# Four graph layers on one core: per-node columns stored as rows after an on-chip transpose, and three transfers moved to other queues

## The chip, the cores and the metric

The kernel runs on one core of a Trainium2 chip. Its time is device microseconds (us) from start to end of one execution, and the smaller the better. One profiled execution with all instructions and all transfers is at hand beside the times.

The engines are named as the profile names them: PE is the matrix engine (PEld its weight loads), DVE the vector engine, ACT the scalar engine, POOL the general engine, SP the engine that only issues transfers. A transfer (DMA) is started by an instruction in the queue of SP, ACT or POOL; the transfers themselves run on 16 DMA engines that all queues share.

## The reference

`adj` is a sparse matrix of 2708 x 2708 (stored dense, with weights), `x` is 2708 x 512. Four layers follow each other; each ends with a layernorm of its input plus its result. Cut to what matters:

```python
deg = max((adj != 0).sum(-1), 1)                       # used in layer 3
# layer 0
head = (adj > 0) / sqrt(count of adj > 0 in the row)   # counts per row
x = layernorm(x + ((adj + head) @ x) / rowsum(adj + head))
# layer 1
h = x @ W_sa
s_left, s_right = h @ a_sa[0, :512], h @ a_sa[0, 512:]      # one score per node
e = where(adj != 0, exp(-leaky_relu(s_left[:, None] + s_right[None, :])), 0)
x_a = (e / (rowsum(e) + 1e-5)) @ h
x_b = adj @ (x @ W_gcnb) + b_gcnb
x = layernorm(x + sigmoid(gate_a(adj @ x, x) * x_a + gate_b(adj @ x, x) * x_b))
# layer 2: p = x; three hops p = adj @ p, each times a weight, summed
# layer 3
dinv = rsqrt(deg)
x = layernorm(x + relu((dinv * (adj + I) * dinv @ x + x) @ W + b))
```

So two things per node are made once and used much later: the two score columns of layer 1 (`rcol` below, which the kernel's third sweep adds to its exponent) and the reciprocal degree (`rdeg`, used in the last sweep).

## The kernel before

The nodes are split into two halves of 1354 and the columns of an output into ranges of 384, 384, 256 and 330. The products with `adj` use the seven-product (Strassen-Winograd) scheme on 2 x 2 blocks, so that sums and differences of adjacency blocks are needed as well. A function `sweep` does one product of the whole matrix: the first sweep is layer 0, the second is `adj @ x` of layer 1 (profile: about 430 to 815 us), the third the attention product of layer 1, and four more (`sweep2`) do the three hops and layer 3. Work is put in a list with a position, sorted, and emitted; the framework makes the order of each engine's queue and all waits from it. Each engine takes its queue strictly in order.

The loads of the adjacency, on the queue of SP, and the sums of blocks, which the second sweep also stores (`save`) for the hops:

```python
def load(ij, k):
    t = ring_tile("a" + ij)                    # one of 38 buffers
    nc.sync.dma_start(out=t[:, :n], in_=adjT[j0 : j0 + P, hi * NH + R0 : hi * NH + R0 + n])
    A[r, ij, k] = t

def comb(dst, a, b, op, k):
    nc.vector.tensor_tensor(A[r, dst, k][:, :n], A[r, a, k][:, :n], A[r, b, k][:, :n], op)
    if save:
        nc.scalar.dma_start(out=SD[m][k * P : (k + 1) * P, R0 : R0 + n], in_=A[r, dst, k][:, :n])
```

The matrix products of a sweep, and how a finished sum leaves its PSUM bank (ACT copies it, or DVE adds it):

```python
nc.tensor.matmul(B[home, c][:, :n], X[STAT[p], k][:, c * P : (c + 1) * P], A[r, MOV[p], k][:, :n], ...)
...
def copy_out(nm, home):
    for c in range(2):
        T[nm, c] = tmp(nm)
        nc.scalar.copy(T[nm, c][:, :n], B[home, c][:, :n])
```

The counts of layer 0. While one range is worked on, the count tiles of the next are loaded (`cl`), made into a 0/1 mask on ACT, and counted by small products:

```python
def count_load(R0, n, h, i):
    t = tmp("cl")                              # one of 17 buffers
    move(nc.gpsimd, t[:w, :n], adjT[j0 : j0 + w, h * NH + R0 : h * NH + R0 + n])

def count_mask(R0, n, h, i):
    nc.scalar.activation(m[:w, :n], t[:w, :n], AF.Sign)
    nc.scalar.activation(m[:w, :n], m[:w, :n], AF.Relu)

def count_tile(R0, n, h, i):
    for j, q in enumerate(tiles_of(R0, n)):
        nc.tensor.matmul(cnt[h][:wq, j : j + 1], m[...], ones_bf[:w, 0:1], ...)
```

The scores. `score` (DVE) makes them node tile by node tile, `scores_end` finishes a group of two to four node tiles and stores the two columns of each tile to memory; the reciprocal degrees are stored likewise:

```python
def scores_end(R0, h, ts):
    ...
    for k in ts:
        for j in range(2):
            nc.gpsimd.dma_start(out=SROW[R0, h][j : j + 1, k * P - R0 : ...].rearrange("a i -> i a"),
                                in_=rcol[: wt(k), h * KT + k, j : j + 1])

def end(h):                                    # in the second sweep
    ...
    nc.gpsimd.dma_start(out=DROW[h][0:1, q * P : q * P + wq].rearrange("a i -> i a"), in_=o)
```

A column lies across the partitions, one value of four bytes in each. The third sweep reads `SROW` back as a row, spread over all partitions (`rows`, on SP), the last sweep does so with `DROW`. After the second sweep's range, `done1` needs the finished sums `C` and, for the gates, these small products (`pz`) and a larger one (`ps_d`):

```python
nc.tensor.matmul(pz[:w], C[h, c][:, lo : lo + w], wab_sb[:, c, :], ...)
...
px = dense(lambda c: C[h, c][:, lo : lo + w], W[1], w)
nc.scalar.mul(y[:w], y[:w], gate[:w, t, 1:2])
move(nc.gpsimd, XB[t], y[:w])
```

Of the kernel before, what the change touches and what calls it, by code (L numbers as in the profile page):

```python
# [21 lines left out]
F32 = mybir.dt.float32  # L22
# [3 lines left out]
P = 128  # L26
EPS = 1e-5
NH = 1354
KT = 11
RANGES = [(0, 384), (384, 384), (768, 256), (1024, 330)]  # L30
RANGES0 = [(768, 256), (0, 384), (384, 384), (1024, 330)]
# [27 lines left out]
def wt(k):  # L59
    return min(P, NH - k * P) if k < KT else P  # L60
# [8 lines left out]
def gnn_kernel(ctx: ExitStack, tc: tile.TileContext, x, adjT, w_sa, a_sa, w_gcn, b_gcn, wab, bab, w_hop, w_out,  # L69
               b_out, out):  # L70
    nc = tc.nc
# [9 lines left out]
    small = ctx.enter_context(tc.tile_pool(name="small", bufs=6))  # L81
    psum = ctx.enter_context(tc.tile_pool(name="psum", bufs=1, space=bass.MemoryType.PSUM))
    dram = ctx.enter_context(tc.tile_pool(name="dram", bufs=1, space=bass.MemoryType.DRAM))

    ident = const.tile([P, P], F32, name="ident")
# [13 lines left out]
    gate = const.tile([P, NT, 2], F32, name="gate")  # L99
    rcol = const.tile([P, NT, 2], F32, name="rcol")  # L100
    rdeg = const.tile([P, NT], F32, name="rdeg")
    wab_sb = const.tile([P, 2 * DC, 2], F32, name="wab_sb")
    bab_sb = const.tile([P, 2], F32, name="bab_sb")
    vmat = const.tile([P, DC, 4], F32, name="vmat")
# [4 lines left out]
    def feature(nm):  # L109
# [4 lines left out]
    X0 = [x[h * NH + k * P : h * NH + k * P + wt(k), :] for h in range(2) for k in range(KT)]  # L114
    OUT = [out[h * NH + k * P : h * NH + k * P + wt(k), :] for h in range(2) for k in range(KT)]

    SROW = {(R0, h): dram.tile([2, w], F32, name=f"SR{R0}_{h}", tag=f"SR{R0}_{h}")
            for R0, w in RANGES for h in range(2)}
    DROW = [dram.tile([1, NH], F32, name=f"DR{h}", tag=f"DR{h}") for h in range(2)]

    X2T = {(g, h): dram.tile([D, 2 * n], F32, name=f"X2T{g}_{h}", tag=f"X2T{g}_{h}")
           for g, (_, n) in enumerate(RANGES2) for h in range(2)}
# [3 lines left out]
    SD = {m: dram.tile([NH, NH], F32, name=f"A{m}", tag=f"A{m}") for m in SUMS}  # L126
# [3 lines left out]
    def bcast(src, n):  # L130
        return bass.AP(tensor=src.tensor, offset=src.offset, ap=[[0, P], [1, n]])

    def move(queue, dst, src):

        m = dst.shape[0]
        c = m - m % 16 if m > 16 else m
        queue.dma_start(out=dst[:c], in_=src[:c])  # L137
        if c < m:
            queue.dma_start(out=dst[c:m], in_=src[c:m])

    def ring_tile(nm):
        return pool.tile([P, 384], F32, name=nm, tag="ring", bufs=RING)
# [13 lines left out]
    def bank(nm, shape=None):  # L156
        return psum.tile(shape or [P, D], F32, name=nm, tag="x", bufs=8)
# [6 lines left out]
    def at(pos, fn, hold=False):  # L164

        def go():
            n = len(nc.cur_bb.bb.instructions)
            fn()
            held.update(range(n, len(nc.cur_bb.bb.instructions)))

        events.append((pos, len(events), go if hold else fn))
# [187 lines left out]
    def sweep(base, ranges, prep=None, extra=None, done=None, first=False, late=None, sums=False, save=False):  # L359
        A, spare = {}, {}  # L360
        nk = KW
        for r, (R0, n) in enumerate(ranges):
            plain = first and r == 0
            pb = base + 7 * r - plain
# [20 lines left out]
            def comb(dst, a, b, op, k, n=n, r=r, R0=R0):  # L385
                if dst == "s3":
                    A[r, "s3", k] = ring_tile("s3")
                nc.vector.tensor_tensor(A[r, dst, k][:, :n], A[r, a, k][:, :n], A[r, b, k][:, :n], op)  # L388
                if save:
                    m = dst if dst == "s3" else {("21", "21"): "s1", ("11", "21"): "s2", ("11", "12"): "s4"}[dst, a]  # L390
                    nc.scalar.dma_start(out=SD[m][k * P : (k + 1) * P, R0 : R0 + n], in_=A[r, dst, k][:, :n])
                if sums and (dst, a) in (("21", "21"), ("11", "12")):
                    add_run(R0, int(dst == "21"), n, P, A[r, dst, k])

# [6 lines left out]
            for ij in ("11", "21", "22", "12"):  # L401
                for k in ks:
                    p, f = when[ij]
                    at(pb + p + f * k / nk, lambda ij=ij, k=k, load=load: load(ij, k))
                    if prep is not None:
                        p, f = pw[ij]
# [13 lines left out]
            for k in ks if not plain else ():  # L420
                f = 0.75 * k / nk
# [48 lines left out]
            if plain:  # L470
                for i in range(8):
                    for k in ks:
                        at(pb + i + k / nk, lambda i=i, k=k, step=plain_step: step(i, k))
                    if i % 2:
                        h, e = i // 4, i // 2 % 2
# [54 lines left out]
            for h in (1, 0):  # L530
                ts = list(range(R0 // P, (R0 + n + P - 1) // P))
# [70 lines left out]
    S = [28.0 * s for s in range(8)]  # L602


    row, run, rd = {}, {}, {}
# [3 lines left out]
    def tiles_of(R0, n):  # L609
        return list(range(R0 // P, (R0 + n + P - 1) // P))  # L610

    def count_load(R0, n, h, i):
        w = wt(i % KT)
        t = tmp("cl")
        j0 = (i // KT) * NH + (i % KT) * P
        move(nc.gpsimd, t[:w, :n], adjT[j0 : j0 + w, h * NH + R0 : h * NH + R0 + n])
        cnt[R0, h, i] = t

    def count_rows(R0, i):
# [153 lines left out]
    for k in range(KW):  # L773
        f = k / KT
# [18 lines left out]
        vec[1] = const.tile([P, D], F32, name="vec", tag="vec")  # L793
        nc.scalar.dma_start(out=vec[1], in_=bcast(b_gcn, D))

    at(S[1] - 1.0, start1)
    deg = {}

    def spread_v():
# [20 lines left out]
    def scores_end(R0, h, ts):  # L820
        q = slice(h * KT + ts[0], h * KT + ts[-1] + 1)
        m = len(ts)
        nc.vector.tensor_tensor(sc[:, q, :], sc2[:, q, 0, :], sc2[:, q, 1, :], ALU.add)
        nc.vector.tensor_scalar(neg_s[:, q], sc[:, q, 1], -1.0, None, ALU.mult)
        nc.vector.tensor_scalar(neg_s01[:, q], sc[:, q, 1], -0.01, None, ALU.mult)
        for j in range(2):
            nc.vector.tensor_scalar(gate_x[:, q, j], sc[:, q, 2 + j], bab_sb[:, j : j + 1], None, ALU.add)

        s01 = small.tile([P, 4], F32, name="s01", bufs=2)
        nc.vector.tensor_scalar(s01[:, :m], sc[:, q, 0], 0.01, None, ALU.mult)  # L830
        nc.vector.tensor_tensor(g_col[:, q], sc[:, q, 0], s01[:, :m], ALU.max)
        nc.vector.tensor_tensor(rcol[:, q, 0], g_col[:, q], sc[:, q, 0], ALU.subtract)
        nc.vector.tensor_tensor(rcol[:, q, 1], g_col[:, q], s01[:, :m], ALU.subtract)
        for k in ts:
            for j in range(2):
                nc.gpsimd.dma_start(out=SROW[R0, h][j : j + 1, k * P - R0 : k * P - R0 + wt(k)].rearrange("a i -> i a"),
                                    in_=rcol[: wt(k), h * KT + k, j : j + 1])

    def scores_over():

# [6 lines left out]
    i = 0  # L847
    for R0, n in RANGES:
        for h in (1, 0):
            for k in tiles_of(R0, n):  # L850
                def go(t=h * KT + k):
                    got1[t] = fetch(X1[t])

                at(S[1] + 0.7 + 0.95 * i, go)
                at(S[1] + 1.1 + 0.95 * i, lambda t=h * KT + k, w=wt(k): score(t, w, got1))
                i += 1
            at(S[1] + 1.12 + 0.95 * (i - 1), lambda R0=R0, h=h, ts=tiles_of(R0, n): scores_end(R0, h, ts))
    at(S[1] + 1.13 + 0.95 * (i - 1), scores_over)

    def extra1(pb, r, R0, n, A):  # L860
        ts = tiles_of(R0, n)

        def tally(h, key, w=P):

            a = A[(r,) + key]
            if (R0, h) not in deg:
                deg[R0, h] = d = tmp("deg")
                nc.vector.tensor_scalar(d[:w, :n], a[:w, :n], 0.0, None, ALU.not_equal)
            else:
                d = deg[R0, h]  # L870
                nc.vector.scalar_tensor_tensor(d[:w, :n], a[:w, :n], 0.0, d[:w, :n], ALU.not_equal, ALU.add)  # L871

        for ij, p in (("11", -0.6), ("21", 0.05), ("22", 1.05), ("12", 3.6)):
            for k in range(KW):
                at(pb + p + 0.8 * k / KT, lambda ij=ij, k=k: tally(int(ij[0]) - 1, (ij, k)))
        for h, p in ((1, 2.0), (0, 4.5)):
            at(pb + p, lambda h=h: tally(h, ("r", h), KA))
            at(pb + p, lambda h=h: tally(h, ("r32", h), 32))

        def end(h):  # L880
            d = deg.pop((R0, h))
            ps = bank("ds", [P, 4])
            for i, q in enumerate(ts):
                wq = wt(q)
                nc.tensor.matmul(ps[:wq, i : i + 1], d[:, q * P - R0 : q * P - R0 + wq], ones_f, start=True, stop=True)
            for i, q in enumerate(ts):
                wq = wt(q)
                o = rdeg[:wq, h * KT + q : h * KT + q + 1]
                nc.vector.tensor_scalar(o, ps[:wq, i : i + 1], 1.0, None, ALU.max)
                nc.vector.reciprocal(o, o)  # L890
                nc.gpsimd.dma_start(out=DROW[h][0:1, q * P : q * P + wq].rearrange("a i -> i a"), in_=o)

        at(pb + 2.6, lambda: end(1))
        at(pb + 5.2, lambda: end(0))

    def done1(p0, dp, last, R0, n, h, C, tiles):
        for i, (t, lo, w) in enumerate(tiles):
# [44 lines left out]
    def extra2(pb, r, R0, n, A):  # L942
        def rows(h):
            row[R0, h] = [tmp("row") for _ in range(2)]
            for m in range(2):
                nc.sync.dma_start(out=row[R0, h][m][:, :n], in_=bcast(SROW[R0, h][m : m + 1, :], n))

        def share(o, s, t, w):
            nc.vector.tensor_tensor(o, s, eps_col[:w, t : t + 1], ALU.add)
            nc.vector.reciprocal(o, o)  # L950
            nc.vector.tensor_tensor(o, o, gate[:w, t, 0:1], ALU.mult)

        at(pb - 1.6, lambda: rows(0))
        at(pb - 1.0, lambda: rows(1))
        at(pb + 5.2, lambda: run_sums(R0, n, 0, share))
        at(pb + 4.7, lambda: run_sums(R0, n, 1, share))
# [375 lines left out]
    for n, i in enumerate(list(nc.cur_bb.bb.instructions)):  # L1332
        p = last if n < 3 * strict else done if n in held else {}
# [44 lines left out]
```

## Time and profile before

| | us |
|---|---|
| median of 3 runs | 2961.59 |
| lowest, highest | 2958.91, 2971.53 |
| span of the profiled execution | 2972.7 |
| first to last store of the degree columns (`DR<-rdeg`, 22 transfers) | issued 498.3 to 885.6 |
| first to last store of the score columns (`SR<-rcol`, 44 transfers) | issued 499.9 to 813.3 |
| stores of the block sums (`As<-a` and `As<-s`, 160 transfers, ACT queue) | issued 428.1 to 866.9 |
| loads of all count tiles (`cl<-in_adjT`, 144 transfers, POOL queue) | issued 1.5 to 314.9 |

How the views are to be read: in a row of the waits, the engine and line that waited stand left of the arrow, what ended the wait right of it, then the total in us, how often, and the longest. A row of the windows gives for one stretch its length, then each engine's busy time (with the count of its instructions), the granted PE clock as a share of full speed, the share of time the 16 DMA engines were busy, and GB/s. A row of the timeline gives start, duration, engine, line, operation, tiles and count, and in brackets the idle time before it and what ended that.

### The profile page before, as it was taken

The page shows a single profiled execution, that of the slowest core. Times are in us where ns is not written, and L with a number is a line of the kernel's source. Part 1 is how long each engine was busy: PE and PEld are TensorE (multiplying, and loading weights), DVE is VectorE, ACT ScalarE, POOL GpSimd, SP SyncE. Part 2 cuts the span into 40 slices and gives each one's busy share as a digit, 9 for nine tenths or more (in the row PEclk, how much of TensorE's full clock was granted, in tenths as well). Part 3 has the DMA queues.
Part 4 walks back from the last instruction along what each step waited for, and adds up shares of the span by engine and source line. Part 5 has one row for each costly group of instructions (what it writes and reads, how often), then busy time and mean ns, then how long its engine had stood idle before and what let it go on. Part 6 is the DMA issues. An engine that isn't in the chain of part 4 may idle for free.

```text
span 2972.7 us, 37453 instructions
## 1 busy us (share of the span) xinstructions
PE 2878.5 (97%) x10898; PEld 1862.9 (63%) x10898; DVE 2233.1 (75%) x5666; ACT 568.1 (19%) x1105; POOL 626.1 (21%) x1116
## 2 busy tenths in 40 slices
PE   6999999999799999999999999999999999999997
PEld 4655665556565666776665666666666666665653
DVE  4898788556546866686598787887888877689886
ACT  3654300000026644462100000000000200100001
POOL 1333222011200010122302223031330312512112
PEclk9999999999899999999999999999999999999999
DMA  7676468786864342464667768566675766866652
GB/s 209 185 214 192 130 186 209 153 130 134 154 143 125 104 150 78 146 200 146 208 189 217 218 194 246 169 205 197 203 235 156 224 194 182 245 180 183 177 159 81
DMA packets 385064, 523.85 MB, mean 176 GB/s; under 512 B 66168, under 2 KB 339872, under 8 KB 384860
## 3 DMA queue, kind: packets, MB, share of 16 engines
q1 hardware_dynamic: 295944, 362.26, 43.5%
q0 software_dynamic: 48896, 120.34, 13.2%
q10 hardware_dynamic: 40020, 38.87, 6.3%
q8 instruction: 86, 1.41, 0.2%
q14 instruction: 118, 0.97, 0.1%
HBM read 432.03 MB, written 89.21 MB: 175 GB/s over the span
## 4 chain that ended last, share of the span: by engine, by line
PE 80%; DMA 7%; DVE 6%; issue 4%; POOL 1%; ACT 1%; SPq 0%; POOLq 0%; ACTq 0%; DVEq 0%
PE accu L1116 10%; PE accd L1116 10%; PE accc L1116 10%; PE ps_d L591 9%; PE accc L443 8%; PE accd L443 8%; PE accu L443 8%; PE acca L1116 5%; PE acca L443 3%; PE accr L1187 2%; DMA a<-in_adjT 1%; DVE z L1076 1%; PE acca L452 1%; PE accr L1191 1%; PE accd L452 1%
## 5 line engine op out<-in xcount | busy, mean ns | idle before, releaser
L1076 DVE TENSOR_TENSOR z<-z 128x339 f32<-128x339 f32 (+1 forms) x966 | 457.6, 506 | 13.9 <-PE accu L1116 2.5
L1134 ACT COPY q<-accu 128x338 f32<-128x338 f32 (+1 forms) x84 | 34.3, 443 | 988.7 <-PE accu L1116 988.7
L1116 PE MATMUL accc<-s,t 128*128 128x338 f32 (+1 forms) x644 | 198.6, 453 | 1.0 <-DVE s L1076 1.0
L1116 PE MATMUL accu<-z,t 128*128 128x338 f32 (+1 forms) x644 | 194.9, 448 | 1.4 <-DVE q L1140 1.4
L1116 PE MATMUL accc<-z,t 128*128 128x338 f32 (+1 forms) x644 | 194.4, 448 | 0.0
L1116 PE MATMUL accd<-z,t 128*128 128x338 f32 (+1 forms) x644 | 193.6, 448 | 0.0
L1237 POOL DMA_DIRECT2D Y<-y x192 | 104.8, 552 | 371.4 <-DVE y L1232 338.8
L388 DVE TENSOR_TENSOR a<-a,a 128x384 f32<-128x384 f32 (+2 forms) x330 | 162.2, 516 | 13.6 <-PE accu L443 12.7
L545 POOL TENSOR_TENSOR rstd<-rstd,neg_half 128x1 f32<-128x1 f32 (+3 forms) x92 | 61.9, 673 | 523.7 <-DVE rstd L544 522.7
L1116 PEld LDWEIGHTS accc<-s,t 128*128 128x128 f32 x644 | 121.4, 191 | 66.6 <-issue 9.4
L1116 PEld LDWEIGHTS accd<-z,t 128*128 128x128 f32 x644 | 122.0, 190 | 61.0 <-issue 1.4
L1116 PEld LDWEIGHTS accu<-z,t 128*128 128x128 f32 x644 | 121.4, 190 | 61.8 <-DVE q L1140 1.9
L1116 PEld LDWEIGHTS accc<-z,t 128*128 128x128 f32 x644 | 121.7, 190 | 60.9 <-issue 2.2
L1076 DVE TENSOR_TENSOR s<-z 128x338 f32<-128x338 f32 (+1 forms) x322 | 150.4, 506 | 9.2 <-PE accc L1116 5.7
L1140 DVE TENSOR_TENSOR q<-q,accd 128x338 f32<-128x338 f32 (+1 forms) x112 | 56.4, 504 | 128.5 <-PE accd L1116 128.2
L871 DVE SCALAR_TENSOR_TENSOR deg<-a,deg 128x384 f32<-128x384 f32 (+2 forms) x152 | 75.2, 505 | 74.8 <-DMA a<-in_adjT 74.0
L937 ACT ACTIVATE e<-row,neg_s 128x384 f32<-128x384 f32 (+5 forms) x176 | 100.4, 571 | 90.1 <-DVE e L939 29.1
L938 ACT ACTIVATE f<-row,neg_s 128x384 f32<-128x384 f32 (+5 forms) x176 | 100.0, 568 | 25.7 <-DVE a L940 5.6
L939 DVE TENSOR_TENSOR e<-e,f 128x384 f32<-128x384 f32 (+5 forms) x176 | 87.7, 509 | 22.1 <-ACT f L938 21.4
L137 POOL DMA_DIRECT2D cl<-in_adjT x132 | 71.3, 545 | 132.0 <-ACT mask L630 73.5
L591 PE MATMUL ps_d<-w,q 128*128 128x512 f32 (+2 forms) x192 | 88.4, 606 | 5.1 <-DVE q L1296 3.8
L940 DVE SCALAR_TENSOR_TENSOR a<-a,e 128x384 f32<-128x384 f32 (+2 forms) x160 | 80.4, 510 | 5.4 <-DMA a<-in_adjT 3.3
(594 smaller groups left out, 5915.4 us busy)
## 6 DMA issues: line engine op xcount, KB each, us to landing
z<-As SPq DMA_DIRECT2D x320, 169.5 KB
z<-As SPq DMA_DIRECT2D x320, 169.0 KB
a<-in_adjT SPq DMA_DIRECT2D x240, 192.0 KB
z<-in_adjT SPq DMA_DIRECT2D x240, 169.5 KB
z<-in_adjT SPq DMA_DIRECT2D x240, 169.0 KB
a<-in_adjT SPq DMA_DIRECT2D x120, 165.0 KB
cl<-in_adjT POOLq DMA_DIRECT2D x80, 192.0 KB, 4.3
a<-in_adjT SPq DMA_DIRECT2D x112, 128.0 KB
```

The costliest lines, as they stand in the source:

```text
L137: queue.dma_start(out=dst[:c], in_=src[:c])
L388: nc.vector.tensor_tensor(A[r, dst, k][:, :n], A[r, a, k][:, :n], A[r, b, k][:, :n], op)
L443: nc.tensor.matmul(B[home, c][:, :n], X[STAT[p], k][:, c * P : (c + 1) * P], A[r, MOV[p], k][:, :n], start=bool(start and k == k0), stop=k ...
L591: nc.tensor.matmul(o, lhs(c), r, start=c == 0 and n == 0, stop=c == DC - 1, skip_group_check=True)
L871: nc.vector.scalar_tensor_tensor(d[:w, :n], a[:w, :n], 0.0, d[:w, :n], ALU.not_equal, ALU.add)
L937: nc.scalar.activation(e[:w, :n], row[R0, h][0][:w, :n], AF.Exp, bias=neg_s[:w, t : t + 1])
L938: nc.scalar.activation(f[:w, :n], row[R0, h][1][:w, :n], AF.Exp, bias=neg_s01[:w, t : t + 1])
L939: nc.vector.tensor_tensor(e[:w, :n], e[:w, :n], f[:w, :n], ALU.min)
L940: nc.vector.scalar_tensor_tensor(a[:w, :n], a[:w, :n], 0.0, e[:w, :n], ALU.not_equal, ALU.mult)
L1076: nc.vector.tensor_tensor(d[:, :n], Z[x + (k,)][:, :n], Z[y + (k,)][:, :n], op)
L1116: nc.tensor.matmul(B[home][:, :n], stat(v, k), a[:, :n], start=bool(start and k == 0), stop=k == nk - 1, skip_group_check=True)
L1237: nc.gpsimd.dma_start(out=rows[:, :, f * P : (f + 1) * P], in_=o[32 * f : 32 * (f + 1), : m * P].rearrange("p (b d) -> p b d", d=P))
```

## The change

1. **Columns become rows on chip.** The score columns of a group (two per node tile) and the degree columns of a group are no longer stored column by column. A group's columns are transposed by PE into a PSUM bank, so that each becomes a row of 128 values on one partition; ACT copies the rows to a small tile, and one POOL transfer stores them. `SROW` and `DROW` are laid out and padded to whole rows of 128 for it, the read back of `SROW` follows that layout, and `rdeg` is first set to 1 so that the padding is defined.
2. **The count tiles of the second range** (`RANGES0[1]`, columns from 0) are loaded on the queue of SP, which also carries the adjacency, and no longer on that of POOL. The later ranges' stay on POOL.
3. **The stores of the block sums** go from the ACT queue to the POOL queue.
4. `start1`, which loads a weight matrix on the ACT queue before the second sweep, is now held in the order of the list.

The aim is to write the columns with long pieces in place of single values, and to take transfers off queues whose engine has other work waiting behind them.

```diff
+    nc.vector.memset(rdeg, 1.0)
...
-    SROW = {(R0, h): dram.tile([2, w], F32, ...)
+    SROW = {(R0, h): dram.tile([2 * ((w + P - 1) // P), P], F32, ...)
             for R0, w in RANGES for h in range(2)}
-    DROW = [dram.tile([1, NH], F32, ...) for h in range(2)]
+    DROW = [dram.tile([1, KT * P], F32, ...) for h in range(2)]
...
-                    nc.scalar.dma_start(out=SD[m][k * P : (k + 1) * P, R0 : R0 + n], in_=A[r, dst, k][:, :n])
+                    nc.gpsimd.dma_start(out=SD[m][k * P : (k + 1) * P, R0 : R0 + n], in_=A[r, dst, k][:, :n])
...
-        move(nc.gpsimd, t[:w, :n], adjT[j0 : j0 + w, h * NH + R0 : h * NH + R0 + n])
+        move(nc.sync if R0 == RANGES0[1][0] else nc.gpsimd, t[:w, :n], adjT[j0 : j0 + w, ...])
...
-    at(S[1] - 1.0, start1)
+    at(S[1] - 1.0, start1, True)
...
-        for k in ts:
-            for j in range(2):
-                nc.gpsimd.dma_start(out=SROW[R0, h][j : j + 1, k * P - R0 : k * P - R0 + wt(k)].rearrange("a i -> i a"),
-                                    in_=rcol[: wt(k), h * KT + k, j : j + 1])
+    def to_rows(cols, m, dst):
+        ps = bank("ps_r", [P, P])
+        nc.tensor.transpose(ps[:m], cols, ident)
+        t = small.tile([P, P], F32, name="rows", bufs=2)
+        nc.scalar.copy(t[:m], ps[:m])
+        nc.gpsimd.dma_start(out=dst, in_=t[:m])
+
+    def score_rows(R0, h, ts):
+        q = slice(h * KT + ts[0], h * KT + ts[-1] + 1)
+        to_rows(rcol[:, q, :].rearrange("p k j -> p (k j)"), 2 * len(ts), SROW[R0, h])
...
             at(S[1] + 1.12 + 0.95 * (i - 1), lambda ...: scores_end(R0, h, ts))
+            at(S[1] + 1.6 + 0.95 * (i - 1), lambda ...: score_rows(R0, h, ts))
...
-                nc.gpsimd.dma_start(out=DROW[h][0:1, q * P : q * P + wq].rearrange("a i -> i a"), in_=o)
+        def rows(h):
+            to_rows(rdeg[:, h * KT + ts[0] : h * KT + ts[-1] + 1], len(ts),
+                    DROW[h][0, ts[0] * P : (ts[-1] + 1) * P].rearrange("(k i) -> k i", i=P))
         at(pb + 2.6, lambda: end(1))
+        at(pb + 3.2, lambda: rows(1))
         at(pb + 5.2, lambda: end(0))
+        at(pb + 5.8, lambda: rows(0))
...
-            for m in range(2):
-                nc.sync.dma_start(out=row[R0, h][m][:, :n], in_=bcast(SROW[R0, h][m : m + 1, :], n))
+            m = (n + P - 1) // P
+            for j in range(2):
+                src = SROW[R0, h][j : j + 1, :]
+                nc.sync.dma_start(out=row[R0, h][j][:, : m * P].rearrange("p (k i) -> p k i", i=P),
+                                  in_=bass.AP(tensor=src.tensor, offset=src.offset, ap=[[0, P], [2 * P, m], [1, P]]))
```

More of the change, by code (lines that the diff above doesn't have):

```diff
@@ L115, in gnn_kernel @@
     OUT = [out[h * NH + k * P : h * NH + k * P + wt(k), :] for h in range(2) for k in range(KT)]
-    SROW = {(R0, h): dram.tile([2, w], F32, name=f"SR{R0}_{h}", tag=f"SR{R0}_{h}")
+    SROW = {(R0, h): dram.tile([2 * ((w + P - 1) // P), P], F32, name=f"SR{R0}_{h}", tag=f"SR{R0}_{h}")
             for R0, w in RANGES for h in range(2)}
-    DROW = [dram.tile([1, NH], F32, name=f"DR{h}", tag=f"DR{h}") for h in range(2)]
+    DROW = [dram.tile([1, KT * P], F32, name=f"DR{h}", tag=f"DR{h}") for h in range(2)]
     X2T = {(g, h): dram.tile([D, 2 * n], F32, name=f"X2T{g}_{h}", tag=f"X2T{g}_{h}")
@@ L615, in count_load @@
         j0 = (i // KT) * NH + (i % KT) * P
-        move(nc.gpsimd, t[:w, :n], adjT[j0 : j0 + w, h * NH + R0 : h * NH + R0 + n])
+        move(nc.sync if R0 == RANGES0[1][0] else nc.gpsimd, t[:w, :n], adjT[j0 : j0 + w, h * NH + R0 : h * NH + R0 + n])
         cnt[R0, h, i] = t
@@ L857, in gnn_kernel @@
             at(S[1] + 1.12 + 0.95 * (i - 1), lambda R0=R0, h=h, ts=tiles_of(R0, n): scores_end(R0, h, ts))
+            at(S[1] + 1.6 + 0.95 * (i - 1), lambda R0=R0, h=h, ts=tiles_of(R0, n): score_rows(R0, h, ts))
     at(S[1] + 1.13 + 0.95 * (i - 1), scores_over)
```

## The prediction, made before the changed kernel ran

> **What bounds the kernel now.** I began with the page's first part, the busy time by engine:
>
> ```profile
> PE 2878.5 (97%) x10898; PEld 1862.9 (63%) x10898; DVE 2233.1 (75%) x5666; ACT 568.1 (19%) x1105; POOL 626.1 (21%) x1116
> ```
>
> PE is the bound: of a span of 2972.7 us it is idle for 94 us only. No part of the change takes a matmul away, so all that it can win lies in that idle time and in stretches where PE runs at a lowered clock. The next view is therefore the sums by 50 us windows (columns: busy us of PE, PEld, DVE, ACT, POOL; granted PE clock; DMA share; GB/s). I kept the windows of the first two layers where PE is neither full nor at full clock:
>
> ```profile
> 50.00:100.00 50.00, 44.63 (x292) 34.64 (x290) 31.11 (x86) 36.91 (x88) 11.57 (x22) 1.00 0.55 159
> 100.00:150.00 50.00, 47.05 (x243) 34.32 (x244) 46.04 (x130) 29.38 (x66) 15.20 (x28) 0.93 0.62 190
> ...
> 450.00:500.00 50.00, 48.07 (x163) 29.63 (x164) 43.95 (x153) 4.12 (x12) 15.49 (x28) 0.93 0.79 245
> ...
> 550.00:600.00 50.00, 45.80 (x146) 26.16 (x143) 25.88 (x88) 3.94 (x9) 4.91 (x10) 0.93 0.67 143
> ...
> 750.00:800.00 50.00, 44.77 (x195) 33.88 (x194) 26.42 (x99) 2.50 (x6) 10.46 (x20) 0.93 0.80 132
> 800.00:850.00 50.00, 37.75 (x126) 24.07 (x125) 24.00 (x79) 6.28 (x11) 5.38 (x10) 0.86 0.74 173
> ```
>
> The reader is to see two losses in each row: 50 less the busy time, and 50 times what the clock lacks (0.07 x 50 = 3.5 us, 0.14 x 50 = 7 us). Also that from 550 on the DMA engines are 67 to 80% busy for 132 to 173 GB/s, while at 450 the same share moves 245. Something makes transfers slow there.
>
> What PE waited for, from the waits of PE (total, times, longest):
>
> ```profile
> PE pz L901 <- DVE P1c L504: 16.5, 3, 12.3
> PE cnt L641 <- ACT mask L631: 6.0, 9, 2.0
> PE accu L461 <- ACT U L497: 5.2, 1, 5.2
> ```
>
> The 12.3 us wait lies at 801, one of 3.65 at 573, the one of 5.2 at 758. For what stands behind the second I took the chain of waits between 555 and 585 (start, us, what):
>
> ```profile
> 559.77 13.54 DMA a<-in_adjT
> ...
> 575.69 0.55 DVE P1c L504
> ...
> 577.23 1.44 PE pz L901 x6
> ```
>
> An adjacency tile takes 13.5 us to arrive; DVE, which takes its queue in order, stands at the degree count of that tile, with the sum `P1c` behind it, and PE waits for `P1c`. The timeline of POOL shows what was issued just before, and the list of DMA issues what that costs (KB each, median us to landing):
>
> ```profile
> 554.63 3.18 POOL L836 DMA_DIRECT2D SR<-rcol  x6 [4.52 <-DVE rcol L833]
> ```
>
> ```profile
> XB<-y POOLq DMA_DIRECT2D x20, 256.0 KB, 2.3
> ...
> SR<-rcol POOLq DMA_DIRECT2D x40, 0.5 KB, 10.7
> ```
>
> Half a kilobyte takes almost five times as long as 256 KB on the same queue. The transfers between 554 and 573 by fortieths (0.475 us each) fall from 362 GB/s to 37 or less from 558.8 to 564.9, for all queues together. The same is there at 502 after three degree and five score columns, at 538 after three degree columns, and at 765 after six score columns. The wait at 801 is reached from that last one: the chain between 780 and 830 begins with a block-sum store that lands 17.02 us after 763.72, goes on through adjacency loads of 3.58 and 9.66 us, then DVE's late score work, a weight load on ACT's queue (5.48) and one more adjacency tile. So the column stores are the cause I choose for the waits at 573 and 801, less surely for the second.
>
> The wait at 758 has a second one. ACT's timeline (row: start, us, engine) shows its queue full of stores of block sums, so that a copy out of PSUM comes late:
>
> ```profile
> 738.44 0.65 ACT L497 COPY W<-accc 128x256 f32<-128x256 f32 x2 [14.96 <-DMA As<-a]
> 739.28 23.27 ACTq L391 DMA_DIRECT2D As<-a  x12
> 762.59 0.37 ACT L497 COPY U<-accu 128x256 f32<-128x256 f32 x1 [23.51 <-DVE a L388]
> ```
>
> **What the Trainium skill says.** "DMA: Bandwidth & Descriptors", section Specifications, gives 512 bytes as the smallest piece at line rate, below which the engine reads, modifies and writes. The columns are pieces of 4 bytes, and the trace agrees in direction (10.7 us against 2.3). The same page, section "Issuing engines are not separate DMA queues", says that moving a transfer to another queue saves only the issuing engine's time, so parts 2 and 3 of the change can only help through what stands behind a transfer in its queue. "TensorE: Matmul & The Clock Gate", Part 1, says that an idle window of about 3.4 us halves the clock. The trace agrees: each PE gap of 3.65 us or more in the first two layers has a window at 0.93 or 0.86 after it.
>
> **The change part by part.**
>
> Columns to rows. It removes 44 + 22 = 66 stores of up to 128 values each, and puts 8 + 8 = 16 stores of whole 512-byte rows in their place (one per half and range). Worth, in the second sweep: the three waits 3.65 + 5.2 + 12.3 = 21.1 us, and the clock after them, 3.5 + 3.5 + 7 = 14 us; together 35 us. Costs: 16 transposes. Four transposes of 128 take 0.63 us on PE's timeline in layer 0, so 16 take some 2.5 us, and they do lie on the path, because PE is the bound. 16 small ACT copies lie beside PE's work (ACT is under 8% busy in the windows from 450). Each transpose is placed about half a position (some 7 us) after its columns, so it should not hold PE. The read back of a row comes in two or three pieces per partition in place of one, 16 loads in all, off the path.
>
> Block sums on POOL. 160 issues of 0.54 us (POOL's rate for the column stores: 3.18 / 6 = 0.53) are 86 us on POOL, less (66 - 16) x 0.54 = 27 us. POOL's busy time from 450 to 850 is 60.5 us by the windows, so it ends near 120 of 400 us: not a bound. ACT's copies then no longer stand behind stores. This belongs to the 5.2 us at 758, counted already. Against it: an adjacency buffer comes free only when its store has landed, and POOL's queue has waits of its own (for the gated `y`, for the degree rows).
>
> Count tiles on SP. The gap before 105 consists of waits of 2.0, 1.1, 0.7 and 1.6 us, 5.5 in all, plus 3.5 us of clock: 9 us. The chain from 88 to 105 goes through POOL: layernorm power, store of `X`, then the load of count tiles behind it, 3.2 us for the transfer, then ACT's masks. On SP no store stands ahead of these loads and an issue takes 0.33 us. ACT's own mask work stays, so I take half, 4.5 us.
>
> `start1` held in order: no time of its own.
>
> Sum: 35 us at about 85%, since other waits will show up behind those removed, is 30; plus 4.5; less 2.5: **32 us**, from 2961.6 to about 2930. What follows is three more layers with PE full, so that time won early should stay won.
>
> **The rivals.**
>
> *The stores of block sums, not the columns, clog the DMA engines.* They run through the same time (428 to 867). For it: SP waits most for `As` landings in this stretch (121.6 us at line 379), and the chain to the wait at 801 holds one. Against it: between 450 and 500 there are 25 such stores and 245 GB/s. If true, the change keeps the clog and only wins the wait behind ACT: about 2950.
>
> *POOL's order becomes the new wait.* A store of a sum waits in POOL behind one that waits for ACT's `y` or for a row copy; its buffer stays taken, the next adjacency load waits in SP, and DVE starves as now. For it: SP already waits for these landings. Against: DVE and POOL each have half of their time free. It would give back some 15 us, about 2945, and at worst, with layernorm's power steps held up at the start of layer 1 (the gap at 448), 2975.
>
> *SP blocks.* Count tiles wait for one of 17 buffers and the adjacency of the next range stands behind them. Against it: in that part of the list SP has little else. It would cost 5 to 10 us.
>
> *More than I count.* All PE time lost between 50 and 850, by the windows shown, is 31 us idle and 24.5 us of clock, 56 in all. Winning all would give 2908.
>
> **Range and chances.** The point is 2930. The low end, 2908, is the whole loss won back with nothing paid; the high end, 2956, is a small net gain, with one rival true. Faster by 2% means below 2902, more than all the loss I found: 0.05. Slower by 2% would take 59 us of new waits: 0.02. Within 2%: 0.93.
>
> **What would show it.** Right: from 500 to 850 no dips under 40 GB/s, landing of the row stores under 5 us, no PE wait over 2 us for `P1c` or `U`, clock 1.00 in the windows from 550 to 850, the first pass of the third sweep some 30 us earlier. The masks' waits at 94 to 105 mostly gone. Wrong: dips that stay without column stores (first rival), POOL or SP waiting long for `As` landings with PE waiting for DVE (second), a new PE wait at `ps_r`, or a gap at 448 much longer than 3.7 us. I may be wrong above all in the order that the framework makes of the new list: it can move waits that no row above shows.

## The result, and the profile after

The changed kernel takes 2926.61 us (2924.77 to 2928.07), the kernel before on the same chip 2966.4: a ratio of 0.9868, with a 95% interval of 0.984 to 0.9895. That is 40 us less, and 3.4 us below the point of the prediction.

The first part of the page after:

```profile
PE 2866.8 (98%) x10914; PEld 1856.8 (63%) x10914; DVE 2234.4 (76%) x5667; ACT 571.5 (20%) x1121; POOL 661.3 (23%) x1178
```

PE is idle for 59.5 us of a span of 2926.3, where it was 94. The same windows as before (length, busy us of PE, PEld, DVE, ACT, POOL, granted PE clock, DMA share, GB/s); everything lies some 10 us earlier now, so the loss at the border of the first two sweeps falls into 400 to 450:

```profile
50.00:100.00 50.00, 41.94 (x268) 32.70 (x268) 31.11 (x92) 41.35 (x96) 2.46 (x4) 0.95 0.67 198
...
400.00:450.00 50.00, 46.42 (x196) 30.94 (x195) 43.10 (x110) 0.67 (x3) 25.98 (x47) 0.97 0.79 250
...
550.00:600.00 50.00, 50.00 (x165) 28.99 (x164) 28.60 (x96) 4.95 (x11) 13.48 (x25) 1.00 0.56 179
...
750.00:800.00 50.00, 50.00 (x202) 34.48 (x201) 30.56 (x98) 7.67 (x14) 18.23 (x34) 1.00 0.52 166
800.00:850.00 50.00, 50.00 (x196) 33.66 (x195) 19.82 (x53) 11.37 (x18) 8.07 (x15) 1.00 0.53 158
```

From 450 to 850 every window is at full clock, and PE lacks 1.3 us in one of them. In the three late windows shown the DMA engines move 158 to 179 GB/s with a share of 52 to 56%; in the same windows before, they were 67 to 80% busy for 132 to 173. Cut into 140 slices of 2.5 us, the stretch from 500 to 850 has 25 slices before in which the DMA engines were busy for over half of the time and moved less than 60 GB/s. After, and with the columns alone (first run below), it has none. A low rate by itself, the sign that the prediction named, says little: 23 slices after lie under 60 GB/s too, with the engines idle for half of the time or more.

The waits of PE (total, times, longest) have lost the rows for `P1c` before `pz` and for `U`; what stays of the first two layers is:

```profile
PE pr L671 <- DVE r L663: 4.8, 3, 2.7
PE cnt L643 <- ACT mask L633: 4.6, 8, 2.0
...
PE ps_n L575 <- DVE P1c L505: 3.5, 1, 3.5
...
PE ps_r L840 <- DVE rcol L835: 1.3, 1, 1.3
```

And the view of the tile `SR` gives what a store of score rows costs now, its count and then its time from issue to landing:

```profile
L843 POOL DMA_DIRECT2D SR<-rows x8: 516/524/524, 496.1 to 783.6; - x8
...
DMA to landing us min/median/max: 1.8/3.0/4.9
```

To see where the 40 us lie, three events that every trace has divide the span: PE's wait before `ps_n` of `P1c` (the transposes of the first sweep's last sum, taken as the start of the second sweep), its first wait of about 4 us before an `accr` of the hops, and the end.

| profiled execution, us | to the start of the second sweep | second and third sweep | hops to the end | span |
|---|---|---|---|---|
| before | 448.3 | 1131.2 | 1393.3 | 2972.7 |
| after | 438.0 | 1100.4 | 1387.9 | 2926.3 |
| difference | 10.3 | 30.8 | 5.4 | 46.4 |

Each border is the start of a wait, that is, the start in the row less the wait in its brackets. The two rows of the trace before, then those of the trace after:

```profile
451.93 0.88 PE L574 MATMUL ps_n<-ident,P1c 128*128 128x128 f32 x2 [3.66 <-DVE P1c L504]
...
1583.86 2.36 PE L1187 MATMUL accr<-r,B11R 116*128 116x338 f32 x4 [4.43 <-DVE q L1198]
```

```profile
441.47 0.74 PE L575 MATMUL ps_n<-ident,P1c 128*128 128x128 f32 x2 [3.50 <-DVE P1c L505]
...
1542.29 2.62 PE L1206 MATMUL accr<-r,B11R 116*128 116x338 f32 x4 [3.91 <-DVE q L1217]
```

The profiled execution of the kernel before was slower than its median by 8 us (2974.5 against 2966.4), which is why the stages add up to more than 40. The part from the hops to the end, which the change hardly touches, differs by up to 10 us between the traces of this study, so its 5.4 us are not put down to the change.

### The profile page after: what moved, and what is told of

Read it like the earlier page. It is cut to its first block, busy times and chain, and to the rows that moved or that the text cites. A ratio compares the mean times of both kernels' runs of the same rounds, so it can differ in the third digit from the quotient of the medians.

```text
span 2926.3 us, 37538 instructions
## 1 busy us (share of the span) xinstructions
PE 2866.8 (98%) x10914; PEld 1856.8 (63%) x10914; DVE 2234.4 (76%) x5667; ACT 571.5 (20%) x1121; POOL 661.3 (23%) x1178
## 4 chain that ended last, share of the span: by engine, by line
PE 84%; DVE 6%; issue 4%; DMA 3%; POOL 1%; SPq 1%; ACT 0%; POOLq 0%; DVEq 0%; ACTq 0%
PE accu L1135 11%; PE accd L1135 11%; PE accc L1135 11%; PE ps_d L592 9%; PE accd L444 9%; PE accu L444 8%; PE accc L444 8%; PE acca L1135 5%; PE acca L444 4%; PE accr L1206 2%; DVE z L1095 1%; PE accr L1210 1%; PE accd L453 1%; PE ps_t L581 1%; PE pz L917 1%
## 5 line engine op out<-in xcount | busy, mean ns | idle before, releaser
L1135 PEld LDWEIGHTS accc<-s,t 128*128 128x128 f32 x644 | 122.1, 192 | 65.9 <-issue 10.3
L882 DVE SCALAR_TENSOR_TENSOR deg<-a,deg 128x384 f32<-128x384 f32 (+2 forms) x152 | 74.0, 502 | 30.8 <-DMA a<-in_adjT 30.2
L392 POOL DMA_DIRECT2D As<-a x120 | 65.0, 544 | 111.5 <-DVE a L389 103.6
```

Source lines behind the costliest of these rows:

```text
L392: nc.gpsimd.dma_start(out=SD[m][k * P : (k + 1) * P, R0 : R0 + n], in_=A[r, dst, k][:, :n])
L1135: nc.tensor.matmul(B[home][:, :n], stat(v, k), a[:, :n], start=bool(start and k == 0), stop=k == nk - 1, skip_group_check=True)
```

## The experiments

Each run was compared with the kernel before on the same chip; that kernel's median was 2977.2 in the first group, 2972.0 in the second and 2965.5 in the third, so ratios are compared, and times only within a group.

**First group: one part of the change at a time.** *Columns alone* is the changed kernel with the other parts undone:

```diff
-                    nc.gpsimd.dma_start(out=SD[m]...)            # block sums back on ACT
+                    nc.scalar.dma_start(out=SD[m]...)
-        move(nc.sync if R0 == RANGES0[1][0] else nc.gpsimd, t...) # count tiles back on POOL
+        move(nc.gpsimd, t...)
-    at(S[1] - 1.0, start1, True)
+    at(S[1] - 1.0, start1)
```

> Theory 1 (single values written to memory slow down every transfer that runs beside them): with the columns alone turned into rows, the second sweep loses its three PE waits at 573, 758 and 801 and some 30 us; the start stays as it was. About 2933 us, 2926 to 2940. Rival (the stores of the block sums on ACT's queue are what hurts): they are still there, so 2950 or more.

Measured: 2941.4 us, ratio 0.9876 (0.9855 to 0.9897), 35.8 us less than before. Second and third sweep took 1101.1 us, 30.1 less than before and within 1 us of the changed kernel.

*Block sums alone* is the kernel before with one line changed:

```diff
-                    nc.scalar.dma_start(out=SD[m][k * P : (k + 1) * P, R0 : R0 + n], in_=A[r, dst, k][:, :n])
+                    nc.gpsimd.dma_start(out=SD[m][k * P : (k + 1) * P, R0 : R0 + n], in_=A[r, dst, k][:, :n])
```

> Only the block-sum stores move to POOL's queue; columns stay single values. Theory 1: transfers are slowed as before, DVE still starves; only the wait behind ACT at 758 (5 us and 3.5 us of clock) can go, so 2950 to 2962. Rival (block sums on ACT's queue are the cause): 2930 to 2940.

Measured: 2959.68 us, ratio 0.9941 (0.9921 to 0.9961), 17.5 us less than before: more than theory 1 allowed (at most 11.6 below the 2961.6 it counted from), and less than the rival asked (21.6 to 31.6). The two sweeps took 1117.9 us, 13.3 less. The wait at 758 is gone; those at 573 and 801 stay, with 2.45 and 8.98 us.

*Count tiles alone*:

```diff
-        move(nc.gpsimd, t[:w, :n], adjT[j0 : j0 + w, ...])
+        move(nc.sync if R0 == RANGES0[1][0] else nc.gpsimd, t[:w, :n], adjT[j0 : j0 + w, ...])
```

> Only the second range's count tiles move to SP's queue. In the trace after, the first product of adjacency tiles comes at 24 us in place of 32. Theory 1a: the twelve count tiles that POOL loads from 1.5 us on took DMA time from the first operands, so this part alone gives some 8 us: 2951 to 2956. Rival a: those 8 us come from elsewhere (another order of the list), and this part alone gives under 2 us.

Measured: 2964.33 us, ratio 0.9956 (0.9943 to 0.9969). The second sweep began 9.8 us earlier (438.5), and 4.9 us of that were lost again in the two sweeps (1136.1 us), where the waits at 573 and 758 had grown to 5.8 and 8.8 us.

*All but the columns* is the kernel before with the two edits above and `start1` held:

> The whole change without its first part: columns still single values, block sums on POOL, count tiles on SP, weight load held. Theory 1: only the start's 8 us and a little of the wait at 758, so 2944 to 2955. Rival (block sums on ACT's queue): near the changed kernel, 2926 to 2932.

Measured: 2957.88 us, ratio 0.9932 (0.991 to 0.9953). The start is as short as in the changed kernel (437.8), the two sweeps take 1120.9 us, and PE waits 7.15 and 7.74 us for `P1c`. `start1` was not tried by itself.

What tells the theories apart is one row of the waits from 430 to 860 us: DVE's degree count waiting for an adjacency tile. Before, columns alone, block sums alone, and all but the columns, one fence for each:

```profile
DVE deg L871 <- DMA a<-in_adjT: 74.0, 29, 10.8
```

```profile
DVE deg L881 <- DMA a<-in_adjT: 32.5, 16, 6.5
```

```profile
DVE deg L871 <- DMA a<-in_adjT: 71.8, 25, 6.7
```

```profile
DVE deg L871 <- DMA a<-in_adjT: 76.6, 21, 9.9
```

It falls to less than half with the columns as rows, and in no run without them; the changed kernel has 30.2. So most of the slow loading comes from the column stores. The block sums matter in two ways. From ACT's queue they hold up ACT's copies while transfers are slow (the wait at 758, which goes with them). And a second row of DVE's waits for adjacency tiles (line 868, the first count of a range and half) nearly goes when they move to POOL's queue; before, and block sums alone:

```profile
DVE deg L868 <- DMA a<-in_adjT: 24.8, 3, 12.1
```

```profile
DVE deg L868 <- DMA a<-in_adjT: 1.5, 1, 1.5
```

The parts do not add up (36 + 17.5 + 13 us alone, 40 together): the first two remove or shorten the same PE waits. What the third is worth beside them stays open (third group).

**Second group: what it is about a column.** *Row by row* keeps the transposes of the changed kernel, but stores each row by itself:

```diff
-        nc.gpsimd.dma_start(out=dst, in_=t[:m])
+        for i in range(m):
+            nc.gpsimd.dma_start(out=dst[i : i + 1], in_=t[i : i + 1])
```

> The changed kernel, but each transposed row goes out in a transfer of its own: 66 stores of 512 bytes, each in 16 pieces of 32 bytes, against 16 stores. Theory 1 (pieces of 4 bytes, some 8,000 of them, are what clogs): 1,056 pieces of 32 bytes cost little, at most 6 us over the changed kernel, a ratio to the kernel before of 0.987 to 0.989. Rival (66 transfers of their own with their fixed cost): back to the kernel without rows, a ratio of 0.993.

Measured: 2932.02 us, ratio 0.9859 (0.9842 to 0.9875). One of its four executions took 3759.1 us at a granted clock of 0.753, and the ratio is without it. As many transfers as before, and nothing of the cost: it isn't the number of transfers.

*Extra columns* adds the old stores to the changed kernel, into memory that nothing reads (the degree columns likewise):

```diff
+        for k in ts:
+            for j in range(2):
+                nc.gpsimd.dma_start(out=DX[R0, h][j : j + 1, k * P - R0 : k * P - R0 + wt(k)].rearrange("a i -> i a"),
+                                    in_=rcol[: wt(k), h * KT + k, j : j + 1])
```

> The changed kernel with the 66 column stores of single values added again, to memory that nothing reads; rows stay as they are. This measures the disputed cost by itself. Theory 1: the second sweep's DVE waits for adjacency tiles come back, two PE gaps of 2 to 8 us with clock loss, 10 to 25 us more: a ratio to the kernel before of 0.991 to 0.996. Rival (the columns only hurt through what waits for them, that is, the read back or POOL's order): nobody reads these, so a ratio of 0.986 to 0.988.

*Extra columns, spaced* does the same with `DX` and `DY` of 128 values per node, of which the first is written:

```diff
+                nc.gpsimd.dma_start(out=DX[R0, h, j][k * P - R0 : k * P - R0 + wt(k), 0:1],
+                                    in_=rcol[: wt(k), h * KT + k, j : j + 1])
```

> As the run with added columns, but each value goes to a row of its own, 512 bytes from the next. If single values clog because many of them fall into the same 512 bytes and have to wait for each other there, this costs far less: landing under 5 us and a ratio to the kernel before of 0.987 to 0.989. If the small size alone is what costs, landing stays near 10 us and the time is that of the run with added columns.

Measured: 2963.21 us and a ratio of 0.9968 (0.9955 to 0.998) for the first, 2934.57 us and 0.9869 (0.9854 to 0.9884) for the second. The first is a little above the range expected. The added columns cost 29 us more when their values lie side by side than when they lie 512 bytes apart. The time from issue to landing of the 44 added stores of score columns, first and second run:

```profile
DMA to landing us min/median/max: 8.1/11.2/16.6
```

```profile
DMA to landing us min/median/max: 1.6/2.5/6.6
```

DVE's wait for adjacency tiles, again first and second:

```profile
DVE deg L889 <- DMA a<-in_adjT: 77.3, 21, 15.2
```

```profile
DVE deg L890 <- DMA a<-in_adjT: 32.4, 20, 6.0
```

Same count of values, same size, same engine, same place in the list; only the place in memory differs. Nor does the split of a store differ: both traces record the added stores as 960 packets of 32 bytes, eight values each, and 96 of 20. Of the 140 slices from 500 to 850, 12 are busy and under 60 GB/s in the first run, none in the second. So single values are not slow here because they are small, but because a whole column goes into the same few hundred bytes. POOL's timeline of the first run shows a second effect: two block-sum stores wait 3.8 and 9.0 us for columns before them to land (in brackets):

```profile
554.75 0.54 POOL L395 DMA_DIRECT2D As<-a  x1 [3.81 <-DMA DX<-rcol]
...
565.88 0.56 POOL L395 DMA_DIRECT2D As<-s  x1 [9.01 <-DMA DX<-rcol]
```

In all, eight such waits take 36.5 us there; the trace of the spaced run has one, of 3.2 us. The 29 us hold both effects, the slow transfers and the waits in POOL's queue, and no run parts them. The kernel before, with its block sums on ACT's queue, has no such waits in POOL's.

*Counts held* is the kernel before with a small copy on POOL that waits for the first row of counts:

```diff
+                    if r == 0 and h == 0 and i == 0:
+                        def gate_pool():
+                            g = small.tile([P, 1], F32, name="gp", bufs=1)
+                            nc.gpsimd.tensor_copy(g, row[R0, 0][:, 0:1])
+                        at(q - 0.7001, gate_pool)
```

> The kernel before, with one small POOL copy put ahead of its count loads that waits for the first range's row of counts (at about 31 us). The count tiles stay on POOL's queue but do not run beside the first operands. Theory 1a (DMA time at the start): the first adjacency product comes at 24 to 25 us, as with the tiles on SP's queue, and the whole gains 6 to 10 us, a ratio of 0.997. Rival a (it is the queue of SP that helps): the start stays at 32 us, ratio 1.000 or more.

Measured: 2970.37 us, ratio 0.9992 (0.9982 to 1.0003). The two halves of the expectation part: in the trace the first products come early, and the second sweep begins 7.8 us sooner (440.5), but no gain is left in the time. Its profiled execution took 2963.7 us, among its fastest, so the other executions are slower somewhere; where was not seen.

**Third group: the start once more, without columns, and one step further.** *Changed kernel again*:

> The changed kernel once more, as the yardstick for the three beside it: a ratio to the kernel before of 0.985 to 0.989.

Measured: 2926.22 us (2923.44 to 2928.61), ratio 0.9871 (0.9856 to 0.9886).

*Block sums back on ACT*, otherwise the changed kernel (first edit of the columns-alone diff):

> The changed kernel with the block-sum stores back on ACT's queue. In the trace of the columns-alone run the second sweep is as short as in the changed kernel, so once the single values are gone the queue of these stores should not matter: within 3 us of the changed kernel. Rival (ACT's copies wait behind stores even so): 5 to 10 us more.

Measured: 2933.56 us (2930.2 to 2938.14), 7.3 us over the changed kernel with ranges that do not overlap. My expectation of 3 us at most fell, and the rival's size was right. The trace shows where for 4 us only: the two sweeps took 1104.6 us, with 3.4 us of half clock at 781; and the next run, which has these stores on ACT's queue too, took 1099.6 us for them. So where the 7.3 us lie stays open.

*Rows, counts held on POOL* is columns alone with the copy of the held-counts run:

> Rows, block sums on ACT, and the second range's count tiles on POOL but held until 25 us by a small copy that waits for the first row of counts. Without single values the second sweep is quiet, so the start can be told apart. Theory 1a (early count tiles take DMA time from the first operands): within 3 us of the run that has rows and these tiles on SP, start at 24 us. Rival a (SP's queue itself matters): 6 us or more above it.

Measured: 2932.56 us (2929.57 to 2935.89), 1.0 us from the run before it, which has the tiles on SP. The first adjacency product on PE's timeline (start, duration, then the wait before it in brackets), before, after, columns alone, and this run:

```profile
31.98 5.49 PE L452 MATMUL acca<-a,B11A 128*128 128x256 f32 x12 [1.38 <-DVE a L688]
```

```profile
24.19 5.49 PE L453 MATMUL acca<-a,B11A 128*128 128x256 f32 x12 [1.38 <-DVE a L690]
```

```profile
32.78 1.65 PE L453 MATMUL acca<-a,B11A 128*128 128x256 f32 x3 [1.38 <-DVE a L689]
```

```profile
25.39 5.06 PE L453 MATMUL acca<-a,B11A 128*128 128x256 f32 x11 [1.38 <-DVE a L689]
```

What the two runs at 32 have in common is on POOL's timeline of the kernel before:

```profile
1.47 4.45 POOL L137 DMA_DIRECT2D cl<-in_adjT  x8 [0.16 <-issue]
```

From 1.5 us on POOL loads count tiles that are not wanted before 66 us, 2.2 MB within the first 11 us (11 x 192 KB, 96 and 15). At the 260 GB/s that all queues moved up to 32 us, that is by estimate 8.7 us of everyone's DMA time, and the first products are 7.8 us later. Held back on POOL or queued behind the first operands on SP, the tiles no longer do this; for the start it makes little difference which queue carries them (25.4 and 24.2 us).

What the early start is worth in the time of the whole stays open. Count tiles alone gained 12.9 us. But in the same group all but the columns, which has them too, took only 1.8 us less than block sums alone, and counts held gained nothing clear (0.9992). And columns alone, which starts at 32.8, has a ratio of 0.9876, no worse than the 0.9897 of the two runs here that differ from it mainly in the early start; it ran in another group, on another chip, and was not run beside them.

*Later spread* moves one step of the changed kernel:

```diff
-                at(pb + p + d + 0.15, lambda h=h: spread_row(R1, n1, h))
+                at(pb + p + d + (0.6 if r == 0 and h == 0 else 0.15), lambda h=h: spread_row(R1, n1, h))
```

> The changed kernel with one step moved: the transposes that spread the second range's first row of counts come some 7 us later in the list. In the trace after, PE waits 2.7 us for DVE there and then runs 6.8 us at half clock. If that wait costs what it seems to, 4 to 6 us less than the changed kernel, ratio to it 0.998; if another wait takes its place, no difference.

Measured: 2922.98 us (2921.52 to 2924.08), ratio to the kernel before 0.986 (0.9845 to 0.9875), 3.2 us below the changed kernel beside it. The wait of 2.7 us is gone from PE's waits, and the window from 50 to 100 has its full clock:

```profile
50.00:100.00 50.00, 44.07 (x291) 34.23 (x291) 31.88 (x94) 41.33 (x95) 2.46 (x4) 1.00 0.70 210
```

It is the fastest kernel of the study, though its range and that of the changed kernel overlap, and the 3.2 us are less than the 4 to 6 expected. The changed kernel beside it has the waits of 2.0 and 2.7 us as well, but only 3.4 us of half clock after them.

## Why the prediction was right, and where it was not

- **Columns to rows, 30 us of 35:** right in size and cause. The two sweeps are 30.8 us shorter after, 30.1 with the columns alone. All three waits and the clock losses after them went; the only new wait is one of 1.3 us at `ps_r`.
- **Why a column is slow:** the prediction took it to be the small size, from the 512 bytes that the Trainium skill names ("DMA: Bandwidth & Descriptors", section Specifications). The size alone is not it: the spaced columns are as small, land in 2.5 us against 11.2, and cost nothing that the times show.
- **The wait at 801:** put down to the column stores "less surely". It went with the columns alone (no wait of PE over 0.7 us from 470 to 1550 in that run), and stayed at 8.98 us with the block sums alone.
- **Block sums on POOL:** that their gain was counted already held for the two sweeps (1099.6 to 1104.6 us in three traces with rows and them on ACT, 1100.3 to 1101.2 in three with them on POOL). In time they gave 7.3 us more beside the rows, a term that the sum lacked, and which no stage of the traces explains. POOL's busy time from 450 to 850 is 109 us by the windows, against the 120 foreseen.
- **Count tiles on SP, 4.5 us from the gap before 105:** this step failed: the place was wrong. That gap is still there, with waits of 2.0 and 2.7 us, and 6.8 us of half clock. The chain of waits after, between 82 and 108, shows DVE's run of sums in front of PE's `pr` in place of POOL's queue:

```profile
94.24 0.43 DVE run L685
94.67 0.21 DVE r L655 x3
...
95.95 0.90 PE pr L671 x3
```

  What the traces do gain came at the start, 7.8 us, in a stretch whose windows I had not listed because all of it looked like waiting for the first operands. It was, but POOL's loads beside them were to be seen.
- **Costs:** the 16 transposes take 0.27 us each on PE by the profile, 4.4 us if none overlaps its neighbours, and made it wait 1.3 us once. The 2.5 us foreseen were on the low side, and no run measured them by themselves.
- **The rivals:** the stores of block sums as the main clog fell with the columns-alone run, in which they stayed where they were. SP's waits for their landings at the adjacency loads fell there to a third, so most of these had been an effect of the slow columns (before, then columns alone, 430 to 860):

```profile
SPq L379 <- DMA As<-a: 121.6, 27, 20.0
```

```profile
SPq L380 <- DMA As<-a: 42.9, 15, 9.0
```

  POOL's order as a new wait shows only where columns are added (9.0 us at 565.9). SP did stand still for the count tiles (19.4 us up to 150, at most 3.1 us at a time), without a wait of PE for the adjacency behind it.
- **The sum:** 32 us predicted, 40 measured. By the stages the time up to the second sweep gave 10.3 us where its step had 4.5; as the worth of the early start is open, so is how the 8 us between are made up. One of the prediction's sums was wrong: the clock losses in the windows shown make 21 us, not 24.5, so that all loss was 53 us and not 56. The low end of 2908 fits the 53. Its reading of the clock holds for the gaps at 448, 573, 758 and 801; it left out a wait of 4.0 us before the first products, whose window shows 1.00, and the half clock after shorter waits (last section).

## What to carry to other kernels

A per-node column that lies across partitions is better transposed on chip before it is stored; if it must go out as single values, give each a place 512 bytes from the next. When transfers of all queues slow down together, look for a store issued a few us earlier with a landing time out of proportion to its size. And look at what a queue with nothing to wait for issues at the very start: loads that are wanted much later take DMA time from the first operands.

## What the runs showed of the hardware

I had not expected that the place of single values would decide everything: the stores of score columns, up to 128 values of 4 bytes each, land in 11.2 us (median) when the values are neighbours, and slow down the transfers of other queues; they land in 2.5 us when the values are 512 bytes apart, with no cost to be seen in the time of the kernel (ratio 0.9869, against 0.9868 of the changed kernel without them). Between them lies the row-by-row store, in unbroken pieces of 32 bytes, which cost nothing to be seen either (0.9859). What in the memory makes neighbours wait was not tried; nor was a distance between 4 and 512 bytes.

PE's clock was halved after shorter waits than I had counted with: in the trace after, 6.8 us at half speed come with two waits of 2.0 and 2.7 us that lie some 7 us apart. The repeat of the same kernel has the same waits and 3.4 us at half speed, and without the second wait (later spread) there is none. Even before, the window from 100 to 150 stood at 0.93 with no wait over 2.04 us ahead of it. So in these traces short waits close together were enough, and how long the clock stayed halved varied from one execution to the next.
